# Expert weights fetched by SyncE at register addresses instead of by GpSimd gathers

## The chip, the cores and the metric

The kernel runs on one core of one Trainium2 chip. The core has five engines with instruction queues of their own: TensorE (PE in the profile, with PEld for the loading of its weights), VectorE (DVE), ScalarE (ACT), GpSimd (POOL) and SyncE (SP). Sixteen DMA engines serve all of them. A DMA is issued by an instruction in an engine's queue, and lands later. The metric is the device time of one execution in microseconds (us), as the median of several runs.

## The reference

One layer of a Perceiver in fp32. 256 latents of width 512 pass through three blocks, each added to the latents after a layernorm of its input:

1. Cross-attention to 4096 context rows and to the latents themselves: 16 query heads, 4 key and value heads of 128, RMS-normed queries and keys with rotary positions, softmax, output projection.
2. A Mamba-2 block: input projection, causal convolution of width 4, a state-space scan in chunks of 128, gated RMS norm, output projection.
3. A mixture of experts: 32 experts of inner width 192, of which each token uses six, and one shared expert of width 384.

Only the third block is touched. It computes

```python
scores = jax.nn.sigmoid(x @ gate_w)
topk_w, topk_i = jax.lax.top_k(scores, TOP_K)                     # 6 of 32
topk_w = topk_w / (jnp.sum(topk_w, axis=-1, keepdims=True) + 1e-20)
combine = jnp.sum(jax.nn.one_hot(topk_i, N_EXP) * topk_w[..., None], axis=1)
act = jax.nn.silu(jnp.einsum('td,edf->tef', x, wg)) * jnp.einsum('td,edf->tef', x, wu)
routed = jnp.einsum('tef,efd,te->td', act, wd, combine)
shared = (jax.nn.silu(x @ sg) * (x @ su)) @ sd
return routed + shared
```

Which tokens go to which expert is known only when the gate has been computed on the chip.

## The kernel before, in words

**Stages.** The cross-attention takes the context in chunks of 512 rows and fills most of the span (scores L748, exponentials L754, products with the values L774). The Mamba block follows. The experts' stage runs from about 807 us to the end.

**Slots.** The kernel computes a token's row only for the experts that it has chosen. The 32 experts are worked through as 16 pairs, one pair a round. Pairs 0 to 3 are experts 0 to 7, fixed when the kernel is built (`FIXED`). The other 24 experts are sorted into 24 slots (`NSLOT`) by how many tokens they have; `places` (L1250) finds the order with a few VectorE operations and a matmul whose result `ps_place` (L1267) holds, on every partition, the expert's number for each slot. Pairs 0 to 4 are wide: each expert has a block of 128 token rows. In pairs 5 to 15, the narrow ones, two experts share one block.

**Weights.** A pair's weights are three tiles: two of 128 x 2048 (1.05 MB each: gate, up, and the first 128 rows of down, of one expert each) and one `rest` tile of 128 x 512 (0.26 MB: the last 64 rows of down of both experts, one on each half of the partitions). There is room for six pairs (`NHELD`). `load_pair` (L1414) takes the place of the pair six before; in the loop it stands after the `down` that read that pair last. The tiles lie in memory that earlier stages used, so the trace calls them by old names (`w_in`, `w_out`, `lacc`, `wkv`, `ctx`, `v`, `kT`, `oacc`).

`load_weights` (L1402) loads the fixed pairs by plain DMAs of SyncE. For the others, `rows_at` (L1392) issues a gather on GpSimd: an indirect DMA that takes, for each of the 128 partitions, a row number from a column of a table in SBUF. The table `place` (128 x 36, unsigned) is made by `place_rows` (L1325): expert x 128 + partition for each of the 24 slots, and, for the 12 rest tiles, expert x 64 plus the partition folded into its half (`fold`, L1191). So there are three gathers a pair and 36 in all, 0.94 to 0.95 us of POOL each.

**A round.** TensorE transposes the block of token rows (`turn`, L1601), multiplies it with gate and up (`gate_up`, L237 in wide rounds, L1629 in narrow ones, into `ps_egu`); ACT takes the silu (L1631), VectorE multiplies it with the up half into `hid` (L1633, L1635); TensorE transposes that (`hidTp`, L1641) and multiplies with down (`ps_ye`, L1651, L1652, L1700); ACT copies the result to `y_sb`. For pairs 0 to 10 ACT then issues a DMA that stores `y_sb` to a buffer `ye` in DRAM (L1660 in narrow rounds): 16 stores of 256 KB. For pairs 11 to 15 `y_sb` stays in SBUF, and TensorE spreads it to the tokens with matmuls into `total` (L1670).

The token rows `xg_sb` come from a DRAM copy of the normed latents by gathers on GpSimd's queue (`fetch`, L1587). When the last store to `ye` has landed, 12 further gathers on that queue (`gather`, L1552, its DMA in L1557) bring the stored results `yk` back, one for each of two token tiles and six choices, and VectorE adds each to `x_sb` with its weight (`add`, L1565). Six tile buffers hold them, with two more borrowed for the last two. `finish` (L1811) adds `total`, and SyncE stores the output (L1814).

**What sets the order.** The source gives every engine its instructions in program order, but the framework's scheduler orders them anew by its own estimate of times, subject to data dependences and to `tc.issue_after(x)`, which keeps what stands under it behind `x`. Before the loop, the loads of pairs 4 and 5 are chained in this way behind the first token rows on GpSimd's queue (`begun`). Each DMA signals one of eight completion semaphores of its kind (eight for the hardware queues of SP and ACT together, eight for GpSimd's), taken in turn, and a DMA waits until the one eight before it in that turn has landed.

The loop over rounds, cut to what matters here:

```python
for n in range(NP):
    gate_up(n)
    ...
    if n + 1 < NP:
        main.turn(n + 1)
    if 0 < n <= LAST:
        down(n - 1)
    elif n > LAST:
        main.down_here(n - 1)
    ...
    if n >= NP - 3:
        add_behind(n, ...)
    if n > 0:
        load_pair(n - 1 + NHELD)
    ...
    turn_hidden(n)
```

Of the kernel before, what the change touches and what calls it, by code (L numbers as in the profile page):

```python
# [12 lines left out]
U32 = mybir.dt.uint32  # L13
I32 = mybir.dt.int32
AF = mybir.ActivationFunctionType
ALU = mybir.AluOpType
AX = mybir.AxisListType
PSUM = bass.MemoryType.PSUM

P = 128  # L20
L = 256
NT = L // P
# [24 lines left out]
NE = 32  # L47
FE = 192
FSH = 384
TOPK = 6  # L50
FT = FSH // P
REST = FE - P
# [4 lines left out]
FIXED = 8  # L57
HALFP = P // 2
# [3 lines left out]
HEAD = 4  # L62
EARLY = 4
TAIL = 10
NW = (FIXED + WIDES) // 2
LAST = NP - TAIL // 2
NSLOT = NE - FIXED
NB = FIXED + WIDES + (NSLOT - WIDES) // 2
NPL = NSLOT + NSLOT // 2
ZROW = (NW + LAST) * P  # L70
NOROOM = 2 * NE * P

# [12 lines left out]
def perceiver_layer(ctx: ExitStack, tc: tile.TileContext, a: dict, out: bass.AP):  # L85
    nc = tc.nc
# [63 lines left out]
    def layer(ctx, bounded):  # L150
# [16 lines left out]
        i8 = keep.tile([P, NT, 8], U32, name="i8")  # L167
        row = keep.tile([P, NT, TOPK], U32, name="row")
        row_y = keep.tile([P, NT, TOPK], U32, name="row_y")
        place = keep.tile([P, NPL], U32, name="place")  # L170
        listed = keep.tile([P, NB], U32, name="listed")
        token = keep.tile([P, NT], FP, name="token")
        crowded = keep.tile([1, 1], I32, name="crowded")
# [1 line left out]
        def carve(tl, *shapes):  # L175

            dims = " ".join(f"d{i}" for i in range(len(tl.shape) - 1))
            tl = tl if len(tl.shape) == 2 else tl.rearrange(f"p {dims} -> p ({dims})")
            out, at = [], 0
            for shape in shapes:  # L180
                n = int(np.prod(shape))
                v = tl[:, at:at + n]
                at += n
                if len(shape) == 2:
                    v = v.rearrange("p (a b) -> p a b", b=shape[1])
                elif len(shape) == 3:
                    v = v.rearrange("p (a b c) -> p a b c", b=shape[1], c=shape[2])
                out.append(v)
            assert at <= tl.shape[1]
            return out  # L190
# [114 lines left out]
        kv = {}  # L305
# [374 lines left out]
        for f in (of_heads[0], *key_turns[0:1], of_heads[1], *key_turns[1:2], last_first,  # L680
# [4 lines left out]
            turn = f()  # L685
# [488 lines left out]

        def routing_memory():
            r = carve(lacc[:, 1], (P,), (P,), (NT, NE), (NT, NE), (NT, NE), (NT, NE), (NT, NE), (NT, 8), (NT, 8),
                      (NT, TOPK), (NT, TOPK), (NT,), (NT * TOPK, NE), (FT, L), (1,), (NE,), (1,), (1,), (NE,), (NE,), (2, NE), (2,), (1,),
                      (NSLOT + 1,), (2, NSLOT + 1))
            names = ("iota", "before", "gate", "ev", "mask", "rank", "dst", "m8", "idx", "rowf", "w8", "den", "hot", "act",
                     "p", "free", "key", "pos", "keys", "at", "base", "value", "fold", "turn", "table")  # L1180
            m.update(zip(names, r))
            m["hot"] = m["hot"].rearrange("p (t k) e -> p t k e", t=NT)
            G.iota(m["iota"], pattern=[[1, P]], base=0, channel_multiplier=0, allow_small_or_imprecise_dtypes=True)
            G.iota(m["p"], pattern=[[0, 1]], base=0, channel_multiplier=1, allow_small_or_imprecise_dtypes=True)
            V.tensor_scalar(m["free"], ident[:, 0:NE], 1.0, None, ALU.mult)
            V.memset(m["free"][:, 0:FIXED], 0.0)
            V.tensor_tensor(m["before"], upper, ident, ALU.subtract)

        def place_tables():

            V.tensor_scalar(m["fold"], m["p"], float(HALFP), -float(HALFP), ALU.is_ge, ALU.mult)  # L1191
            V.tensor_tensor(m["fold"], m["fold"], m["p"], ALU.add)

            def steps(to, first, *by):
                to = to if len(by) == 1 else to.rearrange("p (a b) -> p a b", b=by[1][1])
                G.iota(to, pattern=[list(b) for b in by], base=first, channel_multiplier=0, allow_small_or_imprecise_dtypes=True)

            turn, rows, room, w = m["turn"], m["table"][:, 0], m["table"][:, 1], WIDES + 2 * MIXED
            for to, at0, step, more, narrow in ((turn, 0, 1, NSLOT - MIXED - WIDES, 1), (rows, FIXED * P, P, P - QUARTER, HALFP)):
                steps(to[:, 0:WIDES], at0, (step, WIDES))  # L1200
                steps(to[:, WIDES:w], at0 + WIDES * step, (step, MIXED), (more, 2))
                steps(to[:, w:NSLOT], at0 + (WIDES + MIXED) * step, (narrow, NSLOT - w))
            steps(room[:, WIDES:w], QUARTER, (0, MIXED), (P - HALFP, 2))
            V.tensor_scalar(rows[:, NSLOT:], m["p"], float(P), None, ALU.mult)
            G.memset(turn[:, NSLOT:], float(NSLOT))
            G.memset(room[:, 0:WIDES], 0.0)
            G.memset(room[:, w:NSLOT], float(HALFP))
            G.memset(room[:, NSLOT:], 0.0)
# [40 lines left out]

        def places(pc):  # L1250

            pos, key, keys, at, value, drawn = (
                m[n] for n in ("pos", "key", "keys", "at", "value", "dst"))
            n, low = NSLOT, slice(FIXED, NE)
            two = lambda ap, k: ap.unsqueeze(1).to_broadcast([P, 2, k])

            V.scalar_tensor_tensor(keys, pc[:, 0:NE], float(NE), m["iota"][:, 0:NE], ALU.mult, ALU.subtract)
            V.tensor_scalar(keys, keys, float(2 * NE), None, ALU.add)  # L1258
            V.tensor_tensor(at, keys, m["free"], ALU.mult)
            V.tensor_reduce(key, at, AX.X, ALU.add)  # L1260
            V.tensor_scalar(at[:, 0:n], keys[:, low], key, None, ALU.is_gt)
            V.tensor_reduce(pos, at[:, 0:n], AX.X, ALU.add)

            slot = at[:, 0:n + 1]
            V.tensor_scalar(slot, m["turn"], pos, None, ALU.is_equal)
            ps = bank("ps_place")
            TE.matmul(ps[:, 0:n], number, slot[:, 0:n], start=True, stop=True)  # L1267
            V.tensor_tensor(drawn[:, :, 0:n + 1], m["table"], two(slot, n + 1), ALU.mult)
            V.tensor_reduce(value, drawn[:, :, 0:n + 1], AX.X, ALU.add)
            V.tensor_tensor(drawn, two(ident[:, 0:NE], NE), value.unsqueeze(2).to_broadcast([P, 2, NE]), ALU.mult)  # L1270
            TE.matmul(ps[:, NE:3 * NE], ones, drawn.rearrange("p a b -> p (a b)"), start=True, stop=True)
            V.tensor_copy(expert, ps[:, 0:n])
            place_rows()
            V.tensor_copy(m["base"], ps[:, NE:3 * NE].rearrange("p (a b) -> p a b", b=NE))

        def result_rows():
# [40 lines left out]
        def list_early(es):  # L1317
# [3 lines left out]
                for t in range(NT):  # L1321
                    TE.matmul(ps[:, e:e + 1], first[:, t, e, :], token[:, t:t + 1], start=(t == 0), stop=(t == NT - 1))
            V.tensor_copy(listed[:, es.start:es.stop], ps[:, es.start:es.stop])

        def place_rows():  # L1325


            n, p = NSLOT, m["p"]
            V.tensor_scalar(place_f[:, 0:n], expert, float(P), p, ALU.mult, ALU.add)
            e2 = expert.rearrange("p (n i) -> p i n", i=2)  # L1330
            for i, half in enumerate((slice(0, HALFP), slice(HALFP, P))):
                V.tensor_scalar(place_f[half, n:], e2[half, i], float(REST), m["fold"][half], ALU.mult, ALU.add)
            V.tensor_copy(place, place_f)

        def picks(t, es):

# [52 lines left out]

        held, rests, weights = [], [], {}  # L1390

        def rows_at(out, src, c, by=place):  # L1392

            return G.indirect_dma_start(out=out, out_offset=None, in_=src,  # L1394
                                        in_offset=bass.IndirectOffsetOnAxis(ap=by[:, c:c + 1], axis=0)).ins
# [6 lines left out]
        def load_weights(to, n, fixed, behind=None):  # L1402

            if fixed:
                for i in range(2):
                    wait_for(nc.sync.dma_start(to[i], a["experts"][2 * n + i]), behind)
                nc.sync.dma_start(to[2], a["down_rest"][2 * n:2 * n + 2].rearrange("e p n -> (e p) n"))
            else:
                s = 2 * n - FIXED
                for i in range(2):  # L1410
                    rows_at(to[i], a["experts"].rearrange("e p n -> (e p) n"), s + i)
                return rows_at(to[2], a["down_rest"].rearrange("e p n -> (e p) n"), NE - FIXED + s // 2)

        def load_pair(n, behind=None):  # L1414
            if n < NP:
                k = n % NHELD
                weights[n] = (held[2 * k], held[2 * k + 1], rests[k])
                return load_weights(weights[n], n, 2 * n < FIXED, behind)

        def hold(*tiles, behind=None):  # L1420

# [30 lines left out]
        for fs in plan:  # L1452
# [44 lines left out]
        nc.sync.dma_start(xd[0:P, :], xn[:, 0, :])  # L1497
        assemble(1)
        n = NE - FIXED
        pick, number, expert, place_f, member, own, members = carve(  # L1500
            m["kv", 1], (NT * HEAD, P), (P,), (n,), (NPL,), (TAIL, NE), (TAIL, NE), (4 * TAIL,))
        pick = pick.rearrange("p (t e) r -> p t e r", t=NT)
        turn_latents = lambda t: turn_xn(t, bank("lnT"), halves=True)
        place_tables()
# [205 lines left out]
        with ExitStack() as rctx:  # L1710
# [37 lines left out]
            for n in range(2):  # L1748
                begun = main.fetch(n)
            for n in range(FIXED // 2, NHELD):  # L1750
                with tc.issue_after(begun):
                    begun = load_pair(n)
            copied = main.turn(0)
            with tc.issue_after(copied):
                rows_in_blocks(at)
# [155 lines left out]
```

## Time and profile before

| what | value |
|---|---|
| runs | 940.9, 943.85, 940.94 us; median 940.94 us |
| profiled execution | 946.23 us; span 944.3 us |
| TensorE busy | 924.2 us, 98% of the span |
| VectorE, ACT, POOL busy | 577.4, 370.0, 427.8 us |
| granted TensorE clock | 0.997 |
| bytes of POOL's queue (q0) and SP's queue (q1) | 39.59 MB and 77.43 MB |
| SP's wait for the last `x_sb` before the output store | 62.2 us |

The profile is one execution, recorded by the chip; its span goes from the first to the last instruction. A view of waits lists, for one engine, the idle time before its instructions and what ended it. A timeline row gives start, duration, engine, source line, operation, output and inputs, and in brackets the idle time before it. A row of a stretch gives the busy time of PE, PEld, DVE, ACT and POOL in it, the granted clock, the busy share of the DMA engines and GB/s.

### The profile page before, as it was taken

How to read it: one execution, taken by the hardware profiler on the slowest of the kernel's cores; microseconds unless marked ns; L12 is line 12 of the kernel's file. 1: busy time of each engine (PE TensorE's matmuls, PEld its weight loads, DVE VectorE, ACT ScalarE, POOL GpSimd, SP SyncE). 2: the span in 40 equal slices, each digit the busy share in tenths (PEclk: the TensorE clock that was granted, in tenths of full speed). 3: DMA queues.
4: the chain of work that ended last, by engine and by line, in shares of the span. 5: the costliest groups of instructions: out<-in, count | busy, mean ns of one | idle time of the engine just before them, and what ended most of it. 6: DMA issues, size and time to landing. Idle time of an engine off the chain costs nothing.

```text
span 944.3 us, 10567 instructions
## 1 busy us (share of the span) xinstructions
PE 924.2 (98%) x3266; PEld 504.9 (53%) x3266; DVE 577.4 (61%) x1199; ACT 370.0 (39%) x853; POOL 427.8 (45%) x498
## 2 busy tenths in 40 slices
PE   7999999999999999999999999999999999999996
PEld 3444555555555555555555555554465775654332
DVE  4866766566666665756666656658588685661224
ACT  4556444344344343443444434434154442022121
POOL 3769846345544644724725544220013251545542
PEclk9999999999999999999999999999999999999999
DMA  9651053053024114204305203090025481779983
GB/s 331 203 112 58 1 179 89 1 154 92 1 66 146 33 31 159 57 3 154 90 0 157 68 1 89 14 298 1 0 101 197 145 309 68 288 287 348 421 330 101
DMA packets 129716, 122.33 MB, mean 130 GB/s; under 512 B 79889, under 2 KB 99122, under 8 KB 124402
## 3 DMA queue, kind: packets, MB, share of 16 engines
q1 hardware_dynamic: 118960, 77.43, 27.2%
q0 software_dynamic: 7504, 39.59, 11.3%
q10 hardware_dynamic: 3186, 4.54, 1.3%
q8 instruction: 28, 0.46, 0.2%
q14 instruction: 38, 0.31, 0.1%
HBM read 89.54 MB, written 32.00 MB: 129 GB/s over the span
## 4 chain that ended last, share of the span: by engine, by line
PE 96%; DVE 2%; DMA 0%; issue 0%; ACT 0%; POOL 0%; SPq 0%; ACTq 0%
PE oT L774 24%; PE scT L748 24%; PE ps_kv L522 16%; PE ps_self L237 4%; PE ps_egu L1629 3%; PE ps_o L969 3%; PE ps_egu L237 3%; PE ps_first L399 3%; PE ps_xbc L237 2%; PE ps_out L1163 1%; PE ps_z L237 1%; PE xgTp L1601 1%; PE ps_ye L1651 1%; PE ps_ye L1652 1%; PE total L1670 1%; PE ps_ye L1700 1%
## 5 line engine op out<-in xcount | busy, mean ns | idle before, releaser
L765 DVE TENSOR_TENSOR lacc<-lacc,prT 128x512 f32<-128x512 f32 x256 | 199.8, 781 | 198.0 <-ACT prT L754 196.6
L754 ACT ACTIVATE prT<-scT,bq,rk 128x512 f32<-128x512 f32 x256 | 198.4, 775 | 280.9 <-PE scT L748 268.8
L748 PE MATMUL scT<-qT,kT 128*128 128x512 f32 x536 | 273.5, 592 | 0.0
L774 PE MATMUL oT<-prT,v 128*128 128x512 f32 x528 | 269.4, 592 | 0.0
L774 PEld LDWEIGHTS oT<-prT,v 128*128 128x128 f32 x528 | 100.2, 190 | 125.3 <-issue 118.6
L748 PEld LDWEIGHTS scT<-qT,kT 128*128 128x128 f32 x536 | 101.3, 190 | 41.4 <-issue 30.8
L522 PE MATMUL ps_kv<-fast,ctx 128*128 128x256 f32 x350 | 99.5, 379 | 0.0
L522 PEld LDWEIGHTS ps_kv<-fast,ctx 128*128 128x128 f32 x350 | 66.5, 190 | 47.9 <-issue 39.9
L471 POOL TENSOR_TENSOR ctx<-ctx 128x128 f32<-128x128 f32 x21 | 10.4, 495 | 98.7 <-PE ps_kv L522 98.7
L211 POOL TENSOR_TENSOR rk<-pv,mhalf 128x4 f32<-128x4 f32 x32 | 38.7, 1219 | 27.3 <-DVE pv L210 27.1
L522 PE MATMUL ps_kv<-wkv,ctx 128*128 128x256 f32 x168 | 48.8, 379 | 0.0
L282 ACT ACTIVATE xn<-kraw 128x128 f32<-128x128 f32 x112 | 33.5, 301 | 38.5 <-POOL kraw L497 21.5
L507 POOL TENSOR_TENSOR v<-fast,v 128x768 f32<-128x768 f32 x21 | 40.8, 1958 | 16.5 <-DVE fast L551 15.9
L522 PEld LDWEIGHTS ps_kv<-wkv,ctx 128*128 128x128 f32 x168 | 31.9, 190 | 28.2 <-issue 24.6
L780 DVE TENSOR_TENSOR oacc<-oT,oacc 128x512 f32<-128x512 f32 x64 | 43.7, 682 | 0.0
L1394 POOL DMA_INDIRECT xg_sb<-xd,listed x21 | 20.1, 959 | 31.7 <-DVE lacc L1258 14.4
L522 PE MATMUL ps_kv<-fast,fast 128*128 128x256 f32 x112 | 33.3, 379 | 0.0
L1633 DVE TENSOR_TENSOR hid<-si,ps_egu 128x128 f32<-128x128 f32 x11 | 3.2, 288 | 47.0 <-ACT si L1631 40.0
L522 PEld LDWEIGHTS ps_kv<-fast,fast 128*128 128x128 f32 x112 | 21.3, 190 | 17.8 <-issue 12.0
L288 DVE STREAM_TRANSPOSE tr<-kraw 128x512 f32<-128x512 f32 x28 | 18.3, 690 | 19.6 <-POOL kraw L496 19.6
L469 POOL TENSOR_TENSOR ctx<-fast 128x128 f32<-128x128 f32 x28 | 20.4, 730 | 19.6 <-PE ps_kv L522 19.1
L969 PE MATMUL ps_o<-wo,qT 128*128 128x512 f32 x64 | 28.8, 592 | 0.0
(423 smaller groups left out, 1399.9 us busy)
## 6 DMA issues: line engine op xcount, KB each, us to landing
xg<-xn SPq DMA_DIRECT2D x6, 2560.0 KB
ctx<-in_ctxT_dram SPq DMA_DIRECT2D x7, 1024.0 KB, 4.7
kd<-tr SPq DMA_DIRECT2D x112, 64.0 KB, 2.2
kT<-kd SPq DMA_DIRECT2D x28, 256.0 KB, 2.8
wq<-in_wq_dram SPq DMA_DIRECT2D x4, 1024.0 KB, 10.4
wo<-in_wo_dram SPq DMA_DIRECT2D x4, 1024.0 KB
w_in<-in_W_inT_dram SPq DMA_DIRECT2D x4, 1024.0 KB, 11.7
w_in<-in_experts_dram SPq DMA_DIRECT2D x4, 1024.0 KB, 6.9
```

The source lines that it names most:

```text
L211: return G.tensor_tensor(dst, v[:, :n], mhalf[:, :n], ALU.pow)
L237: last = TE.matmul(ps, lhs(k), rhs_of(k), start=(k == 0), stop=(k == KD - 1))
L282: S.activation(sq[:, h, :], raw[:, h, :], AF.Square, accum_out=ss[:, h:h + 1])
L399: TE.matmul(ps, lhs[:, j, k, :], rhs[:, k, :], start=(start and k == 0), stop=(k == 1), skip_group_check=True)
L507: G.tensor_tensor(to[:, 1:4], q, base[:, 1:4], ALU.add)
L522: TE.matmul(b[n], sets[name][i], y, start=start, stop=True, skip_group_check=True)
L748: scored.append(TE.matmul(sc, kT[:, g, i * P:(i + 1) * P], qT[:, t, heads4(g), :].rearrange("p h q -> p (h q)"), start=True, stop=True).ins)
L754: S.activation(pr, sc, AF.Exp, bias=shift, scale=SCALE if r is None else r[:, i, g:g + 1])
L765: V.tensor_tensor(la, la, pr, ALU.add)
L774: TE.matmul(outs[g, t], v[:, i, g * HD:(g + 1) * HD], pr, start=(n == 0), stop=last)
L780: V.tensor_tensor(ov, outs.pop((g, t)), ov, ALU.add)
L969: TE.matmul(m["ps_o", t], aT[:, t, h, :], wo[j][:, h % 4, :], start=(h == 0), stop=(h == NH - 1))
```

## The change

The table of row numbers goes. Instead the 24 expert numbers are copied as integers into a tile `drawn` on one partition. For each pair that is not fixed, SyncE loads two of these numbers into registers, and issues four DMAs whose DRAM address is computed from a register: two for the experts' large tiles and two for the halves of the rest tile. `load_pair` returns nothing any more, and the chain that held the first loads behind the token rows on GpSimd's queue is dropped with it. The fixed pairs' loads, the token rows and the result rows stay as they are. The local name `drawn` in `places` becomes `each`.

```diff
-        place = keep.tile([P, NPL], U32, name="place")
+        drawn = keep.tile([1, NSLOT], I32, name="drawn")
...
         def place_tables():
 
-            V.tensor_scalar(m["fold"], m["p"], float(HALFP), -float(HALFP), ALU.is_ge, ALU.mult)
-            V.tensor_tensor(m["fold"], m["fold"], m["p"], ALU.add)
...
+            V.tensor_copy(drawn, ps[0:1, 0:n])
             V.tensor_copy(expert, ps[:, 0:n])
-            place_rows()
             V.tensor_copy(m["base"], ps[:, NE:3 * NE].rearrange("p (a b) -> p a b", b=NE))
...
-        def place_rows():
-
-
-            n, p = NSLOT, m["p"]
-            V.tensor_scalar(place_f[:, 0:n], expert, float(P), p, ALU.mult, ALU.add)
-            e2 = expert.rearrange("p (n i) -> p i n", i=2)
-            for i, half in enumerate((slice(0, HALFP), slice(HALFP, P))):
-                V.tensor_scalar(place_f[half, n:], e2[half, i], float(REST), m["fold"][half], ALU.mult, ALU.add)
-            V.tensor_copy(place, place_f)
...
-        def rows_at(out, src, c, by=place):
+        def rows_at(out, src, c, by):
...
                 s = 2 * n - FIXED
-                for i in range(2):
-                    rows_at(to[i], a["experts"].rearrange("e p n -> (e p) n"), s + i)
-                return rows_at(to[2], a["down_rest"].rearrange("e p n -> (e p) n"), NE - FIXED + s // 2)
+                _, es = nc.values_load_multi_w_load_instructions(drawn[0:1, s:s + 2], engines=[mybir.EngineType.SP], min_val=0, max_val=NE - 1)
+                for i, e in enumerate(es):
+                    nc.sync.dma_start(to[i], a["experts"][bass.ds(e, 1)].rearrange("o p n -> (o p) n"))
+                for i, e in enumerate(es):
+                    nc.sync.dma_start(to[2][i * REST:(i + 1) * REST], a["down_rest"][bass.ds(e, 1)].rearrange("o p n -> (o p) n"))
...
-                return load_weights(weights[n], n, 2 * n < FIXED, behind)
+                load_weights(weights[n], n, 2 * n < FIXED, behind)
...
             for n in range(FIXED // 2, NHELD):
-                with tc.issue_after(begun):
-                    begun = load_pair(n)
+                load_pair(n)
```

More of the change, by code (lines that the diff above doesn't have):

```diff
@@ L68 @@
 NB = FIXED + WIDES + (NSLOT - WIDES) // 2
-NPL = NSLOT + NSLOT // 2
 ZROW = (NW + LAST) * P
@@ L1176, in routing_memory @@
             r = carve(lacc[:, 1], (P,), (P,), (NT, NE), (NT, NE), (NT, NE), (NT, NE), (NT, NE), (NT, 8), (NT, 8),
-                      (NT, TOPK), (NT, TOPK), (NT,), (NT * TOPK, NE), (FT, L), (1,), (NE,), (1,), (1,), (NE,), (NE,), (2, NE), (2,), (1,),
+                      (NT, TOPK), (NT, TOPK), (NT,), (NT * TOPK, NE), (FT, L), (1,), (NE,), (1,), (1,), (NE,), (NE,), (2, NE), (2,),
                       (NSLOT + 1,), (2, NSLOT + 1))
             names = ("iota", "before", "gate", "ev", "mask", "rank", "dst", "m8", "idx", "rowf", "w8", "den", "hot", "act",
-                     "p", "free", "key", "pos", "keys", "at", "base", "value", "fold", "turn", "table")
+                     "p", "free", "key", "pos", "keys", "at", "base", "value", "turn", "table")
             m.update(zip(names, r))
@@ L1250, in places @@
         def places(pc):
-            pos, key, keys, at, value, drawn = (
+            pos, key, keys, at, value, each = (
                 m[n] for n in ("pos", "key", "keys", "at", "value", "dst"))
@@ L1267, in places @@
             TE.matmul(ps[:, 0:n], number, slot[:, 0:n], start=True, stop=True)
[L1268 to L1271, printed above, removed]
+            V.tensor_tensor(each[:, :, 0:n + 1], m["table"], two(slot, n + 1), ALU.mult)
+            V.tensor_reduce(value, each[:, :, 0:n + 1], AX.X, ALU.add)
+            V.tensor_tensor(each, two(ident[:, 0:NE], NE), value.unsqueeze(2).to_broadcast([P, 2, NE]), ALU.mult)
+            TE.matmul(ps[:, NE:3 * NE], ones, each.rearrange("p a b -> p (a b)"), start=True, stop=True)
+            V.tensor_copy(drawn, ps[0:1, 0:n])
             V.tensor_copy(expert, ps[:, 0:n])
-            place_rows()
             V.tensor_copy(m["base"], ps[:, NE:3 * NE].rearrange("p (a b) -> p a b", b=NE))
@@ L1499, in layer @@
         n = NE - FIXED
-        pick, number, expert, place_f, member, own, members = carve(
-            m["kv", 1], (NT * HEAD, P), (P,), (n,), (NPL,), (TAIL, NE), (TAIL, NE), (4 * TAIL,))
+        pick, number, expert, member, own, members = carve(
+            m["kv", 1], (NT * HEAD, P), (P,), (n,), (TAIL, NE), (TAIL, NE), (4 * TAIL,))
         pick = pick.rearrange("p (t e) r -> p t e r", t=NT)
```

## The prediction

> **What bounds the kernel now.** I read the page's head first, then the chain that ended last, then TensorE's own waits in the expert stage, and only then the queues and engines that the edit touches.
>
> ```profile
> span 944.3 us, 10567 instructions
> PE 924.2 (98%) x3266; PEld 504.9 (53%) x3266; DVE 577.4 (61%) x1199; ACT 370.0 (39%) x853; POOL 427.8 (45%) x498
> PE 96%; DVE 2%; DMA 0%; issue 0%; ACT 0%; POOL 0%; SPq 0%; ACTq 0%
> ```
>
> TensorE is busy 98% of the span and carries 96% of the chain, so an edit that leaves its work alone can only give or take idle time between matmuls. Its waits from 798 us (the shared expert, routing and all rounds of experts) to the end are these (total, count, longest):
>
> ```profile
> PE total L1670 <- ACT y_sb L1665: 2.1, 1, 2.1
> PE ps_egu L1629 <- DVE xgT L1603: 1.2, 3, 0.4
> PE ps_egu L237 <- DVE xgT L1603: 1.2, 1, 1.2
> PE ps_shared L1384 <- issue: 0.4, 1, 0.4
> ```
>
> None names a weights transfer. That is so although the transfers run without a gap; by stretch (columns: us; busy PE, PEld, DVE, ACT, POOL; granted clock; DMA share; GB/s):
>
> ```profile
> 865.00:912.00 47.00, 45.55 (x348) 16.73 (x346) 9.67 (x30) 10.30 (x25) 22.10 (x25) 1.00 1.02 417
> ```
>
> A narrow round moves 2 x 1.05 + 0.26 MB of weights and 0.52 MB of token rows and results, 2.88 MB, at 417 GB/s 6.9 us, and lasts 5.6 us (two silus of ACT at 905.96 and 911.54). The queue therefore lives on its lead: over the twelve gathered pairs the landings are 5 to 13.5 us after the issue, and the smallest distance from landing to first matmul is 9.3 us (pair 13: 899.4 to 908.7).
>
> **The change part by part.**
>
> *Routing on VectorE.* Here are its rows before the first round, from the timeline (start, duration, what it does; in brackets the idle time before and what ended it), and the matmul that waits for them:
>
> ```profile
> 806.28 0.18 DVE L1272 COPY xc<-ps_place 128x24 f32<-128x24 f32 x1 [1.26 <-PE ps_place L1271]
> 806.51 0.27 DVE L1329 TENSOR_SCALAR xc<-xc,lacc 128x24 f32<-128x24 f32 x1
> 806.65 0.48 DVE L1332 TENSOR_SCALAR xc<-xc,lacc 64x12 f32<-64x12 f32 x2
> 807.30 0.17 DVE L1333 CAST place<-xc 128x36 uint32<-128x36 f32 x1
> 809.31 0.68 DVE L1603 COPY xgT<-xgTp 128x512 f32<-128x512 f32 x1
> 810.04 5.43 PE L237 MATMUL ps_egu<-w_in,xgT 128*128 128x384 f32 x16 [1.16 <-DVE xgT L1603]
> ```
>
> L1329, L1332 and L1333 go (0.27 + 0.48 + 0.17 = 0.92 us, overlapping), a 1x24 copy comes in ahead of L1272 (at most that row's 0.18). The xgT copy cannot start before its transposes (807.85 + 1.04 = 808.89), so at most about 808.95: 0.36 us sooner. Bounds: no gain, and the whole 1.16 us. I take -0.36, since the transposes are a recorded row. The two folding operations of L1191 and L1192 (0.15 us each at 724.9, beside other work) count nothing, at most -0.3.
>
> *Loads on SyncE.* Per pair it gets one load of two values (the load of `crowded` on SP: 0.29 us), register and assert steps (0.16 + 0.02 in that row; four, so 0.35), and four transfers with one register step each: 4 x (0.16 + 0.33, the fixed experts' mean issue) = 1.96. Together 2.6 us in a round of 5.6; twelve pairs take 31 us of an SP that otherwise waits 62.2 us for the last x_sb. Bounds: 0.33 x 4 = 1.3 and, with 0.29 for every step, 3.8 us; both are under 5.6. Pair 4 can start about 807 (806.28 + 0.18 + 0.29 + 0.35), against the first gather at 807.75. Queued behind it on SP are only the next pairs' loads; the `crowded` value, ready at 822.5, sits between pairs 6 and 7, whose buffers come free later. On TensorE: 0, covered by the 9.3 us lead; without it every late microsecond is one.
>
> The fixed experts' loads by SP from 754 to 762 us moved 356 GB/s, 430 in the best two microseconds. At 356 instead of 417 a round's 2.88 MB take 8.1 us, 1.2 more than now: over the seven pairs 9 to 15 8.4 us, still inside 9.3. Cost 0; bounds 0 and, with SP's 2.6 us on top, 8.4 + 2.6 - 9.3 = 1.7.
>
> *The rest tile in two.* Each pair's 0.26 MB becomes two transfers of 64 partitions: 12 more, 0.49 us of SP each, counted above. The Trainium skill, "DMA: Bandwidth & Descriptors", section "Rules for kernel authors", advises against just this: transfers to disjoint partition halves share the same engines and serialize, so one 128-partition transfer should be used. By its figure of about 2.0 us fixed per transfer ("Anatomy of one DMA"), served one after the other, 12 of them would be an estimated 24 us on a full queue, 15 past the lead, near 956 us. The rows speak otherwise, since two 1 MB loads issued 0.4 us apart keep the engines full: transfers in flight overlap, and bytes are unchanged. I take 0.
>
> *GpSimd.* 36 gathers of 0.95 us go, 34 us of POOL, and with them their places in the queue ahead of token rows and result rows. No wait of TensorE names POOL or a token row (those land at least 3.7 us early), so 0. After the first rounds this only matters in the tail.
>
> *Stores of ACT.* Hardware transfers share eight completion semaphores in turn, each waiting for the one eight before. 48 loads now alternate with ACT's 16 stores of y_sb. The closest meeting is pair 5's store behind pair 9's rest: about 861.5 + 10 = 871.5 against a store at 873.1. Behind the store on ACT's queue stands the next silu, with idle of 2.1 to 2.3 us before it. If that load takes 13.5 us (the slowest row) ACT is held 1.9 us. Bounds: 0, all of it inside the idle, and 11.4, none of it so in six narrow rounds; I take 0, by the idle rows, and price the case at half, 5.7.
>
> *The tail.* This is where order changes. TensorE needs `hid` of pairs 14 and 15 from VectorE. Before, pair 14's stands among the six additions of result rows; in the built changed kernel all six stand ahead of it, and the four of the second tile ahead of pair 15's now wait for the last four gathers rather than the next four. The timeline rows that decide, of ACT's queue, POOL, VectorE and TensorE:
>
> ```profile
> 903.61 0.33 ACTq L1660 DMA_DIRECT2D ye<-y_sb  x1
> 900.17 0.94 POOL L1394 DMA_INDIRECT ctx<-in_experts_dram,place  x1 [1.48 <-DMA v<-in_down_rest_dram,place]
> 911.83 0.95 POOL L1557 DMA_INDIRECT yk<-ye,row_y  x1 [8.21 <-DMA ye<-y_sb]
> 918.39 0.94 POOL L1557 DMA_INDIRECT yk<-ye,row_y  x1 [0.30 <-issue]
> 926.83 0.95 POOL L1557 DMA_INDIRECT yk<-ye,row_y  x1 [0.30 <-issue]
> 919.27 0.29 DVE L1633 TENSOR_TENSOR hid<-si,ps_egu 128x128 f32<-128x128 f32 x1 [3.26 <-issue]
> 923.02 0.38 PE L1641 MATMUL hidTp<-ident,hid 128*128 128x128 f32 x2
> 929.77 0.29 DVE L1633 TENSOR_TENSOR hid<-si,ps_egu 128x128 f32<-128x128 f32 x1 [1.35 <-ACT si L1631]
> ```
>
> Count from pair 10's store, 903.61. TensorE comes to pair 14's transpose 19.4 us later and, without the 2.06 us stall, to pair 15's 26.25 us later (931.92 - 2.06). The first row gather starts at T0, here 8.2. The sixth follows 6.56 later, lands in about 3.5 (3.1 to 3.8) and is added in 0.75: T0 + 10.8, with `hid` (0.65) T0 + 11.45. The twelfth follows 13.75 (eleven steps of 1.25) to 15.0 (seen) later: its addition ends at T0 + 18.0 to 19.3, with `hid` T0 + 18.65 to 19.95. With T0 = 8.2: 0.25 us late at pair 14, in all 0.6 to 1.9 at pair 15. With T0 under 6.3 nothing. T0 should be a little sooner, as pair 15's loads, gathers from 897.75 with the second one at 900.17 ahead of the store, now wait for pair 9's store, landing about 905.9; so less lies beside pair 10's store, whose 7.4 us compare with 2.0 for an equal store on quiet queues. Bounds 0 and, at the slowest store (10.3), 4.8; I take +0.4, near the low end of 0.6 to 1.9.
>
> *The 2.06 us stall* belongs to ACT starting a copy 3.4 us after its matmul. In the new order pair 15's gate matmuls (2.6 us) stand between, so such a stall would be hidden: 0 to -2.06. I take 0, since the profiled execution, 946.23 us (span 944.3 and 1.93 around it), is 5.3 above the median 940.94 and the stall may be part of those.
>
> Sum: 946.23 - 0.36 + 0 + 0.4 = 946.3 in the profiled execution; on the median 940.94, **941.0 us**.
>
> **The rivals.**
> - *Hidden anyway* (0.47): the edit does what it says, to work that already had 9 us of lead. 941.0; its own range goes from the whole front wait and no tail cost, 939.8, to the tail's 1.9, 942.5.
> - *VectorE's tail* (0.20, slower): pair 10's store lands late and both `hid` stand behind additions. Past T0 = 9.5 us after the store (at the slower pace) the loss passes 2.8; at a 10.3 us store T0 is 11.1 and the price 11.1 + 19.95 - 26.25 = 4.8, so 945.4. For it: the built order and saturated engines. Against: fewer bytes in flight beside that store.
> - *Stores held by loads* (0.11, slower): the shared semaphores above, to 940.94 - 0.36 + 5.7 = 946.3. For it: strict alternation of two engines' transfers. Against: 1.6 us of slack and ACT's idle.
> - *GpSimd relieved* (0.22, faster): T0 comes early, the 2.06 stall is hidden and the whole 1.16 us at the front goes: 940.94 - 3.2 = 937.7. For it: these are the stage's largest waits. Against: the stall may not exist in the median run.
>
> **How the numbers follow.** About 0.3%, 2.8 us, is what a measurement of this kernel can tell from no change. The first case gives "same", 0.47; the two slower ones 0.31; the last 0.22. The range reaches down to the last case and up to the tail's price, 937.6 to 945.4.
>
> **What would show it.** Right: no wait of TensorE for a weights transfer; the wait before the first gate matmuls near 0.8 us instead of 1.16; POOL about 34 us less busy; the software queue down by some 28 MB and SP's up by as much. T0 decides the tail: a transpose of `hid` (L1641 before) waiting for VectorE, with an addition ending last, makes the second case; silus late behind a held store the third. Wrong altogether would be weights arriving late, seen as waits of the gate matmuls for SP's transfers, or engines at well under 417 GB/s.

## The result: 0.57% slower, and the profile after

The changed kernel takes 948.69 us in the median of twenty runs, against 942.65 us for twenty of the kernel before (the 940.94 us that the prediction started from came from three): a ratio of 1.0057, with a 95% interval of 1.0043 to 1.0071. 941.0 us with a range up to 945.4 was forecast, that is no change; measured are 6.0 us more. The page of its profiled execution (949.46 us), its head, chain and the two queues:

```profile
span 947.7 us, 10759 instructions
PE 924.1 (98%) x3266; PEld 505.8 (53%) x3266; DVE 577.3 (61%) x1194; ACT 369.7 (39%) x853; POOL 392.9 (41%) x462
PE 92%; DMA 3%; DVE 3%; issue 1%; ACT 0%; POOL 0%; ACTq 0%; DVEq 0%
q1 hardware_dynamic: 124336, 105.75, 35.2%
q0 software_dynamic: 3088, 11.27, 3.8%
```

The 28 MB have moved from GpSimd's queue to SyncE's and POOL is 34.9 us less busy. TensorE does the same work, but the chain that ended last now runs through DMA and VectorE too. The waits of TensorE from 780 us on (total, count, longest) say where:

```profile
PE hidTp L1630 <- DVE hid L1622: 5.9, 1, 5.9
PE ps_egu L236 <- DVE xgT L1592: 0.8, 1, 0.8
```

The second line is the front: 0.8 instead of 1.16 us, the 0.36 us of the prediction. The first is new and is the loss: TensorE stands 5.9 us before it can transpose `hid` of pair 14. The timeline of the tail, of ACT's and SyncE's queues, POOL, VectorE and TensorE:

```profile
900.14 0.33 ACTq L1649 DMA_DIRECT2D ye<-y_sb  x1
906.47 0.33 SPq L1399 DMA_DIRECT2D ctx<-in_experts_dram  x1
908.72 0.94 POOL L1546 DMA_INDIRECT yk<-ye,row_y  x1 [15.64 <-DMA v<-in_down_rest_dram]
914.97 0.94 POOL L1546 DMA_INDIRECT yk<-ye,row_y  x1 [0.30 <-issue]
916.54 0.75 DVE L1554 SCALAR_TENSOR_TENSOR x_sb<-yk,lacc,x_sb 128x512 f32<-128x512 f32 x1 [6.66 <-DMA yk<-ye,row_y]
924.12 1.54 DVE L1554 SCALAR_TENSOR_TENSOR x_sb<-yk,lacc,x_sb 128x512 f32<-128x512 f32 x2 [0.25 <-DVE x_sb L1554]
925.57 0.28 DVE L1622 TENSOR_TENSOR hid<-si,ps_egu 128x128 f32<-128x128 f32 x1
925.91 0.83 PE L1630 MATMUL hidTp<-ident,hid 128*128 128x128 f32 x2 [5.90 <-DVE hid L1622]
```

The first row gather starts 8.6 us after pair 10's store, where 8.2 us had been seen before. But it lands 7.3 us after its issue, and the sixth 9.6 us (read from the updates of their semaphores), where those of before took 3.1 to 4.2 us (one of the twelve has no record). So the sixth addition ends T0 + 16.9 us and not T0 + 10.8, and `hid` of pair 14 stands behind it. Beside the gathers, pair 15's second large tile (`ctx`) is still on its way: issued at 906.47 instead of 900.17, landed at 922.2 instead of 913.2. Counted from pair 10's store it is issued 6.3 us behind instead of 3.4 us ahead.

After the wait TensorE comes back slower. By stretch (us; busy PE, PEld, DVE, ACT, POOL; granted clock; DMA share; GB/s), first the changed kernel, then the first two stretches of the kernel before:

```profile
865.00:890.00 25.00, 25.00 (x218) 9.31 (x220) 5.33 (x16) 6.21 (x15) 3.78 (x4) 1.00 1.03 391
890.00:905.00 15.00, 15.00 (x111) 5.67 (x104) 3.99 (x12) 2.71 (x7) 0.94 (x1) 1.00 1.03 368
926.00:930.00 4.00, 3.75 (x12) 1.51 (x14) 3.83 (x6) 0.37 (x1) 0.00 (x0) 0.50 0.22 72
```

```profile
865.00:890.00 25.00, 24.01 (x197) 8.53 (x196) 4.32 (x13) 5.11 (x12) 14.36 (x16) 1.00 1.02 418
890.00:905.00 15.00, 14.55 (x112) 5.42 (x113) 4.00 (x12) 3.67 (x9) 7.56 (x8) 1.00 1.03 419
```

The clock column reads 0.50 from 926 to 930; in the chain pair 15's sixteen gate matmuls take 4.50 us instead of 2.73. The first two rows of each hold a second surprise: the DMA engines are as busy as before (1.03; before 1.02 and 1.03), yet move 391 and 368 GB/s where the kernel before moved 418 and 419.

The sum of the tail, 5.9 + 0.24 (a short wait for `xgT`) + 1.8 (gate matmuls) + 0.45 (the two transposes, 0.83 instead of 0.38), is 8.4 us. Spans differ by only 3.4 us, since the profiled execution of before had itself lost some 3 us by the time it came to this transpose (923.02, against 920.0 here), and then its 2.06 us stall. The medians differ by 6.0, so an ordinary execution of the kernel before seems to lose some 2 us that the changed one does not. The profiles show a candidate. In that of the kernel before, ACT starts the silus of pairs 7, 8 and 9 only 2.1, 1.6 and 1.9 us after their gate matmuls have ended, and these three rounds, from 875 to 895 us, take 6.2 to 6.7 us instead of 5.6. Two such rounds stand in the profiles of e2 and e4 below, none in those of the changed kernel and of e10 (0.1 us). What holds ACT there is not shown.

### The profile page after: what moved, and what is told of

It reads as the page before. It is cut to its first block, busy times and chain, and to the rows that moved or that the text cites. A ratio compares the mean times of both kernels' runs of the same rounds, so it can differ in the third digit from the quotient of the medians.

```text
span 947.7 us, 10759 instructions
## 1 busy us (share of the span) xinstructions
PE 924.1 (98%) x3266; PEld 505.8 (53%) x3266; DVE 577.3 (61%) x1194; ACT 369.7 (39%) x853; POOL 392.9 (41%) x462
## 4 chain that ended last, share of the span: by engine, by line
PE 92%; DMA 3%; DVE 3%; issue 1%; ACT 0%; POOL 0%; ACTq 0%; DVEq 0%
PE oT L773 24%; PE scT L747 24%; PE ps_kv L521 16%; PE ps_self L236 4%; PE ps_o L968 3%; PE ps_egu L1618 3%; PE ps_egu L236 2%; PE ps_first L398 2%; PE ps_xbc L236 2%; PE ps_out L1162 1%; PE ps_z L236 1%; PE ps_ye L1689 1%; PE ps_ye L1641 1%; PE ps_sgu L236 1%; PE xgTp L1590 1%; PE ps_ye L1640 1%
## 5 line engine op out<-in xcount | busy, mean ns | idle before, releaser
L236 PE MATMUL ps_self<-wq,xT 128*128 128x512 f32 x64 | 28.6, 592 | 0.0
```

The source lines that it names most:

```text
L236: last = TE.matmul(ps, lhs(k), rhs_of(k), start=(k == 0), stop=(k == KD - 1))
```

## Experiments

The theory after the result: the loss needs two things at once, row gathers that land late since weights are still in flight, and an order of VectorE that puts `hid` behind the additions that wait for them. Rivals: the order alone, the lateness alone, SyncE's register work, something else in SyncE's transfers. The kernel before took between 940.1 and 943.1 us on the chips used, so ratios, each to the kernel before on the same chip, are compared.

**e1: the order put right.**

```diff
-                if n >= NP - 3:
-                    add_behind(n, *{NP - 3: (0, TOPK), NP - 2: (TOPK, 2 * TOPK - 2), NP - 1: (2 * TOPK - 2, 2 * TOPK)}[n])
+                if n >= NP - 2:
+                    add_behind(n, *{NP - 2: (0, TOPK), NP - 1: (TOPK, 2 * TOPK)}[n], turned)
```

(`turned` is the copy of the next pair's `xgT`; the additions are issued behind it as well.)

> The changed kernel with the additions of result rows put behind hid and the turned token rows: tile 0's six behind pair 14's hid and pair 15's xgT, tile 1's six behind pair 15's hid. Theory (late gathers times order): the 5.9 us wait of hidTp for hid goes, and with it the slower clock after it, about 2 us; 948.69 - 7.9 = about 940.8, ratio to before 0.996 to 1.000. Rival 1 (the order alone is to blame): the same number. Rival 2 (SyncE's transfers themselves cost TensorE time elsewhere): it stays at 947 or more, ratio 1.004 or more.

Measured: 942.46 us, ratio 1.0012 (0.9996 to 1.0027). TensorE's waits:

```profile
PE ps_egu L1618 <- issue: 1.3, 1, 1.3
PE ps_egu L236 <- DVE xgT L1592: 0.8, 1, 0.8
```

The wait for `hid` is gone, the clock stays at 1.00, and the loss is gone. Not all of the expected gain is there (0.996 to 1.000): the 1.3 us stand before the first gate matmul that reads `ctx` (921.40), so pair 15's late tile is now a wait of its own. The view of waits names no cause, but the instruction records do: TensorE's instruction at 921.40 waits for the semaphore that `ctx`'s transfer signals, and the last 8 KB packet of SyncE's loads ends at 920.63. SyncE's transfers cost nothing elsewhere that shows.

**e2: the changed order in the kernel before.**

```diff
+                if n >= NP - 2:
+                    with tc.issue_after(added[TOPK - 1 if n == NP - 2 else 2 * TOPK - 3]):
+                        return self.gated(n, si, ps)
```

(`gated` holds the multiplications that make `hid`, `added` the additions.)

> The kernel before, with hid of pair 14 held behind the six additions of tile 0 and hid of pair 15 behind four of tile 1, as the changed kernel has them. Theory: the gathers still land in 3.1 to 3.8 us, so the sixth addition ends 10.8 us after the first gather and the price is the 0.6 to 1.9 us of the prediction; ratio 1.000 to 1.003. Rival 1 (the order alone): the whole loss appears, about 6 us, ratio 1.006.

Measured: 944.54 us, ratio 1.0021 (1.0012 to 1.0031), a wait of 1.3 us for `hid` of pair 14. Its gathers land in 3.1 to 3.8 us. So the order alone, with gathers that land early, costs some 2 us (1.1 to 2.8 by the interval), close to the 0.6 to 1.9 that the prediction worked out, and not 6.

**e3: no weights beside the row gathers.** Pair 15's weights are not loaded, so that its result is another's.

```diff
+                if n < NP - 1:
-                load_weights(weights[n], n, 2 * n < FIXED, behind)
+                    load_weights(weights[n], n, 2 * n < FIXED, behind)
```

> The changed kernel without the loads of pair 15's weights (it multiplies with what pair 9 left), VectorE's order unchanged. Theory: no weights are in flight beside the result rows, gathers land in 3 to 5 us instead of 7.1 to 9.6, the wait for pair 14's hid falls from 5.9 us to under 1.5; ratio 0.998 to 1.001. Rival 1 (order alone): the wait stays near 5.9, ratio 1.006. Rival 3 (the first gather starts late because of the y stores): gathers land faster but the wait stays above 3 us.

Measured: 943.37 us, ratio 1.0011 (0.9996 to 1.0026). The gathers land in 3.1 to 4.1 us, although the first starts at 908.08 as in the changed kernel (908.72), and with the order unchanged the wait is

```profile
PE hidTp L1631 <- DVE hid L1623: 1.3, 2, 1.1
```

So T0 is not the cause; what lies beside the gathers is. e1, e2 and e3 together: either factor alone costs 0.1 to 0.2% (in e1 and e3 not clear of nothing), both 0.57%.

**e4: the kernel before with the additions behind `hid`** (the edit of e1).

> The kernel before with the additions behind hid as in the first run. Theory: before loses nothing to the additions, so nothing changes beyond the 2.1 us stall for y_sb that its profile shows: ratio 0.998 to 1.000. Rival 1: if order alone is worth much, 0.995 or less.

Measured: 945.9 us, ratio 1.0042 (1.0030 to 1.0055): slower, which neither theory had. TensorE has no new wait, and the output stores are issued 3.9 us earlier than in the profile of before (937.86), yet the span ends only 1.0 us sooner (two views, one line of each):

```profile
span 943.3 us, 10567 instructions
...
933.95 1.12 SPq L1814 DMA_DIRECT2D out_dram<-x_sb  x2
```

What comes last is GpSimd. In the instruction records its last gather, held back by the additions of tile 0 whose buffers it needs, lands at 931.9; then come 4.5 us of clean-up and a drain of 6.1 us to 942.5, while SyncE was done at 939.7. e10 tests that.

**e5 and e6: no registers; then one transfer fewer.** Constant addresses, so that other experts' weights are used, with four transfers a pair (e5), and with the rest tile in one of 128 partitions (e6):

```diff
-                for i, e in enumerate(es):
-                    nc.sync.dma_start(to[i], a["experts"][bass.ds(e, 1)].rearrange("o p n -> (o p) n"))
...
+                for i in range(2):
+                    nc.sync.dma_start(to[i], a["experts"][2 * n + i])
+                for i in range(2):
+                    nc.sync.dma_start(to[2][i * REST:(i + 1) * REST], a["down_rest"][2 * n + i])
```

In e6 the last two lines are

```diff
+                nc.sync.dma_start(to[2], a["down_rest"][2 * n:2 * n + 2].rearrange("e p n -> (e p) n"))
```

> The changed kernel with the same four SyncE transfers a pair from constant addresses, no values loaded into registers; experts are then taken by position instead of by the drawn order, so the weights are other experts' and the bytes the same. Theory: registers cost nothing on the path, so the loss stays: ratio 1.004 to 1.007, hidTp waits 4 to 7 us for hid. Rival (SyncE's register work makes the loads late): the loss goes, ratio 1.000 to 1.002.

> As the run before, but the rest tile of a pair in one transfer of 128 partitions, three a pair instead of four, same bytes. Theory (eight transfers in flight at most, so that four a pair hold the next ones back): the last load is issued 2 to 4 us earlier, the wait for hid falls to 2 to 4 us, ratio 1.002 to 1.004. Rival (bytes in flight alone, the count does not matter): like the run before, 1.004 to 1.007.

Measured: e5 948.81 us, ratio 1.0061 (1.0041 to 1.0082), a wait for `hid` of 5.8 us; the registers are not the cause. e6 943.91 us, ratio 0.9998 (0.9982 to 1.0014), better than the theory had said: no wait for `hid`, `ctx` issued at 900.46 (1.5 us behind pair 10's store), and the rate is back. Its tail still holds two other waits, 1.5 us for `xgT` and 1.2 us for `hidT`. The two stretches of e6:

```profile
865.00:890.00 25.00, 25.00 (x226) 9.31 (x224) 5.33 (x16) 5.99 (x15) 3.79 (x4) 1.00 1.03 418
890.00:905.00 15.00, 15.00 (x106) 5.94 (x104) 3.99 (x12) 3.57 (x9) 0.95 (x1) 1.00 1.02 415
```

(e5 moved 391 and 373.) But e6 takes away two things at once, the fourth transfer and the halves of 64 partitions. e13 parts them.

**e7 and e8: registers for the large tiles, gathers for the rest tiles,** in the changed order (e7) and with the additions behind `hid` (e8).

```diff
-                for i, e in enumerate(es):
-                    nc.sync.dma_start(to[2][i * REST:(i + 1) * REST], a["down_rest"][bass.ds(e, 1)].rearrange("o p n -> (o p) n"))
+                return rows_at(to[2], a["down_rest"].rearrange("e p n -> (e p) n"), s // 2, place)
```

> The changed kernel with the large tiles by SyncE as it has them, and the rest tiles by gathers of GpSimd as before (a table of 12 columns, four VectorE operations more); two hardware transfers a pair. VectorE's order in the tail is the changed one. Theory: SyncE is held back less, pair 15's second tile is issued near 900 instead of 906.5 and lands before most row gathers; the wait for hid falls under 2 us, ratio 1.000 to 1.002. Rival (hardware transfers beside row gathers slow these whatever their time): ratio 1.004 or more.

> The run before with the additions behind hid as in the first run. Theory: neither the wait for hid nor the 1.3 us wait that the first run has before pair 15's second gate matmuls remains: 940.8, ratio 0.997 to 0.999. Rival: something else bounds the tail, ratio 1.000 or more.

Measured: e7 942.17 us, ratio 0.9989 (0.9978 to 0.9999), `ctx` issued at 900.03, a wait for `hid` of 1.1 us. e8 939.31 us, ratio 0.9953 (0.9939 to 0.9968): faster than both kernels. Both ratios are a little better than expected. No wait above 0.3 us is left in e8's tail; the largest from 780 us on is the front's:

```profile
PE ps_egu L237 <- DVE xgT L1602: 1.1, 1, 1.1
```

So the registers and SyncE's queue are usable; the halved rest tile is what does not pay. e13 asks what about it.

**e13: four transfers, no halves.** As e6, with one large tile in two transfers of half the columns.

```diff
+                for j in range(2):
+                    nc.sync.dma_start(to[1][:, j * w:(j + 1) * w], a["experts"][2 * n + 1][:, j * w:(j + 1) * w])
```

> As e6 (constant addresses, rest tile in one transfer of 128 partitions; other experts' weights), with one of the two large tiles in two transfers of 128 partitions and half of the columns each: four transfers a pair as in e5, none of 64 partitions, same bytes. Theory A (the halves of 64 partitions slow the engines): 415 GB/s or more from 865 to 905 us, no wait for hid above 2 us, ratio 0.999 to 1.002, like e6. Theory B (four transfers a pair use up the eight in flight): rate near 370 to 390, wait for hid 4 us or more, ratio 1.004 to 1.007, like e5.

Measured: 941.5 us, ratio 0.9983 (0.9964 to 1.0003), no wait for `hid` (one of 2.4 us for `hidT`), and

```profile
865.00:890.00 25.00, 25.00 (x224) 9.42 (x220) 5.82 (x19) 5.69 (x15) 3.87 (x5) 1.00 1.03 414
890.00:905.00 15.00, 15.00 (x106) 5.82 (x100) 3.50 (x10) 3.24 (x8) 0.85 (x1) 1.00 1.03 412
```

That is Theory A, though rate and ratio lie just under its ranges: four transfers a pair cost nothing, the halves lower the rate. The packets' own times agree. Between 862 and 905 us an 8 KB packet of SyncE takes 0.344 us in the mean in the changed kernel, 0.315 in e6 and 0.314 in e13. How a half slows the others is not shown. In slices of 2 us the changed kernel's mean goes from 0.31 to 0.47, and packets of the halves move in the three slowest, 0.42 to 0.47 at 884, 900 and 908 us (28, 84 and 47 of them); but the slice with the most of them, 113 at 866 us, has 0.31. Nor are two properties of a half parted: it has 64 partitions, and it is small, 128 KB. No run loads the rest tile in two transfers of 128 partitions.

**e9, e12, e14, e15: is the slow clock part of the loss?** Matmuls whose result is overwritten fill TensorE's idle time in the changed kernel, 26 (e9) or 13 (e12, e14) of them; e15 is the changed kernel again.

```diff
+                if n == NP - 2:
+                    for _ in range(13):
+                        TE.matmul(tp.rearrange("p a b -> p (a b)"), ident, spread[:, 0, :], start=True, stop=True)
```

> The changed kernel with 26 matmuls of 128x256 (about 0.215 us each, 5.6 us) whose result is overwritten, put between the last total and the transpose of pair 14's hid, where TensorE otherwise idles 5.9 us. Theory (idle TensorE comes back at a lower granted clock, so pair 15's 16 gate matmuls take 4.5 instead of 2.7 us): the transposes start no later, the clock stays at 1.0 and 1.8 us come back; 946.9 against 948.7, ratio to before 1.003 to 1.005. Rival (the slow matmuls come from something else, as transfers into the tiles they read): they still take 4.5 us, ratio 1.006.

> The run before last but two with 13 matmuls instead of 26, as each proved to be two instructions of 0.215 us, so 5.6 us in all, just less than the 5.9 us of idle. Theory (idle TensorE comes back at a lower granted clock): pair 15's 16 gate matmuls take 2.7 us instead of 4.5 although the wait for hid ends when it did, and 1.8 us come back: 946.9 against 948.7, ratio to before 1.003 to 1.005. Rival (the clock falls anyway, or what is won is lost in a later wait): ratio 1.006.

> The kernel of e12, beside the changed kernel on one chip. Theory (idle TensorE comes back at a lower clock): 1.0 to 2.0 us less than e15. Rival: within 0.7 us of e15.

> The changed kernel itself, as the measure for e13 and e14 on their chip: ratio to before 1.005 to 1.008, wait for hid 5 to 7 us.

Measured: e9 950.91 us, ratio 1.0104 (1.0089 to 1.0120): I had mis-sized the filling, each matmul was two instructions, and 11.2 us of them outlasted the wait. e12 947.46 us, ratio 1.0075 (1.0061 to 1.0088): no gain in the whole time, against another chip's run of the changed kernel. Side by side it is there: e14 946.68 us, ratio 1.0044 (1.0031 to 1.0058), e15 949.16 us, ratio 1.0070 (1.0058 to 1.0082), 2.5 us apart and more than the expected 1.0 to 2.0. The clock itself is plain in the chain of e12 and of e15, the rows of pair 15's gate matmuls, first e12:

```profile
926.58 2.80 PE ps_egu L1618 x16
```

```profile
923.71 4.50 PE ps_egu L1618 x16
```

So this wait, 3.7 us in e15's profile (5 to 7 were expected; it is the fastest of the six runs of e15), costs 1.7 us more than itself. e12's trace also shows the landings of that tail without gaps; the issues from 905 to 930 us, with the time to landing last:

```profile
ctx<-in_experts_dram SPq DMA_DIRECT2D x1, 1024.0 KB, 15.0
v<-in_down_rest_dram SPq DMA_DIRECT2D x3, 128.0 KB, 11.9
yk<-ye,row_y POOLq DMA_INDIRECT x12, 8.2
```

**e10 and e11: GpSimd's end.** e4 and e8 with eight tile buffers for result rows, so that the last gathers need not wait for additions.

```diff
-            yp = rctx.enter_context(tc.tile_pool(name="yp", bufs=6))
+            yp = rctx.enter_context(tc.tile_pool(name="yp", bufs=8))
```

> The kernel before with the additions behind hid, as in the fourth run, and eight tile buffers for result rows instead of six, so that the last row gather need not wait for the sixth addition. Theory (in the fourth run GpSimd's own end, some 14 us after its last gather, came last): the last gather goes 3 to 6 us earlier, GpSimd's end falls below that of the output store, ratio 0.996 to 1.000 instead of 1.0042. Rival (the order itself costs something on TensorE): ratio stays at 1.003 or more.

> The eighth run with eight tile buffers for result rows. GpSimd's end there stands 0.4 us behind nothing but just ahead of the output store. Theory: TensorE's chain bounds it, so nothing changes, ratio 0.994 to 0.997. Rival (GpSimd's end decides in most executions): 0.993 or less.

Measured: e10 940.55 us, ratio 0.9998 (0.9989 to 1.0007): the last gather goes at 923.69 instead of 928.35, and e4's loss is gone. GpSimd's end, 2.8 us behind SyncE's in e4 (942.5 against 939.7), was the larger part of it. It need not be all: e10's profile also lacks the two late rounds of e4's, some 1.5 us. e11 938.58 us, ratio 0.9979 (0.9969 to 0.9989), just outside the expected 0.994 to 0.997: faster than the kernel before, like e8, and not faster than e8 by the ratios; their chips differ, so between these two nothing is decided.

## Why the prediction was wrong, point by point

- **The rest tile in two, taken as 0**, is the step that failed first. I argued that transfers in flight overlap and the bytes are the same. They are, but the halves lower the rate, from 418 and 415 GB/s in e6 and 414 and 412 in e13 to 391 and 373 in e5 and 391 and 368 in the changed kernel. "Engines at well under 417 GB/s" stood among the signs of being wrong altogether, and a lower rate had been priced (356 GB/s), but only against the lead of the weights. The lower rate makes the last weights late: SyncE issues `ctx` 6.3 us behind pair 10's store, where the prediction's landing of pair 9's store (905.9) allowed 2.3 and e6 has 1.5. How it is held is shown by its own waits from 860 to 912 us, of which these are the largest:

```profile
SPq L1401 <- DMA w_in<-in_experts_dram: 8.3, 3, 4.9
SPq L1401 <- DMA ye<-y_sb: 5.6, 4, 3.5
SPq L1399 <- DMA oacc<-in_experts_dram: 4.6, 1, 4.6
SPq L1399 <- DMA ye<-y_sb: 4.5, 1, 4.5
```

  SyncE waits for earlier transfers to land, eight back in the turn of the semaphores (a half of pair 13's rest tile is issued at 896.85, as pair 12's second large tile lands at 896.84), so a lower rate becomes a later issue. The Trainium skill's rule that was weighed there ("DMA: Bandwidth & Descriptors", "Rules for kernel authors": use one 128-partition transfer instead of two to disjoint halves) was right in its direction: the runs show a lower rate with the engines as busy as before. The estimate of 24 us made from its page was not right: the figure of about 2.0 us stands there for transfers that GpSimd issues, these are SyncE's, and e13 with four transfers a pair loses nothing against e6 with three. Why packets slow beside the halves, no run here shows.
- **The tail, taken at +0.4 with an upper end of 4.8**, is the term of the sum that was too small: 8.4 us in the profile. It had the right mechanism, order before `hid`, and a wrong entry: "lands in about 3.5". That came from gathers with little beside them (DMA share 0.62 from 912 to 926 us, against 0.90 in the changed kernel). I saw that pair 15's loads would move away from pair 10's store, and missed that they would move beside the gathers. 7.3 to 9.6 us, in place of 3.5, is the missing 6 us of T0 + 16.9. T0 itself, 8.6 us after the store, was not early as I took it to be, and stayed under the 9.5 us that I had named as the point of decision.
- **The rival "VectorE's tail" (0.20)** is the one that came, by another door: slow gathers, not a late store. Its price of 4.8 also left out the clock: 1.8 us on the gate matmuls.
- **The front** was right: 0.36 us.
- **SyncE's issue work and registers, taken as 0**: right (e5 with constant addresses loses as much). The 2.6 us a pair never reached TensorE.
- **GpSimd, taken as 0**: nearly right; it is 34.9 us less busy, and that moved no wait in the tail. But the token rows that "land at least 3.7 us early" are late once, early in the stage: TensorE waits 0.36 us for `xg_sb` at 826.25 (1.2 us in e3, 1.3 in e9), where the kernel before has no such wait. A gather issued for it at 819.54 takes some 7 us to land, with SyncE's loads in flight; its like before took some 5.
- **ACT's stores held by loads (0.11)**: did not come: pair 10's store is issued 0.6 us after its copy begins, as before, and the silus of pairs 5 to 13 start within 0.1 us of their matmuls' end. The waiting is on the other side, where SyncE waits for stores.
- **The lead of 9.3 us on weights** was more than used up by pair 15. No wait of TensorE names weights in the changed kernel, but only since TensorE was waiting for `hid` at that time: without that wait, in e1, it stands 1.3 us for `ctx`.

## What to carry to other kernels

When transfers are moved, ask not only whether their own user still gets them in time, but what else is in flight when they now run: a latency taken from a quiet stretch of the trace doesn't hold beside them. Be wary of splitting a small tile by halves of the partitions: here a large tile split by columns (e13) and a gather for the small one (e7) kept the rate. Look at GB/s beside the busy share of the engines, since the share alone showed no difference. Where a scheduler orders the queues, read its order for work that waits for DMAs ahead of work that the busiest engine needs, and pin that order: e8 and e11, with large tiles at register addresses, rest tiles gathered and the additions pinned behind `hid`, beat both kernels.

## What the runs showed of the hardware that was not expected

- Two transfers of 64 partitions, 128 KB each, among 1 MB ones: 391 and 368 GB/s at a DMA share of 1.03; the same bytes in transfers of 128 partitions, none under 256 KB: 412 to 418 at 1.02 to 1.03.
- After 5.9 us of idle, and in e15 after 3.7, TensorE's sixteen gate matmuls took 4.50 us instead of 2.73; in the changed kernel the clock granted from 926 to 930 us was 0.50. After the 2.06 us stall of the kernel before they took 2.73. The Trainium skill, "TensorE: Matmul & The Clock Gate", section "What's actually happening", puts the step to half clock at about 3.4 us of idle; these three waits agree with it. A half clock came without such idle too: in the profiles of both kernels the clock is also 0.50 for 3.4 us, from 818.5 us before and from 817.8 us in the changed one, behind 24 matmuls of 17 columns and with no wait above 1.2 us since 800 us. Eight gate matmuls there take 3.84 us in the kernel before; in e8 the same eight take 2.82 and the clock stays at 1.00, behind the same 24. What decides it, no run here shows.
- GpSimd's end grows with the DMAs that it has issued: the last long drain took 6.12 us in the kernel before (69 gathers in the stage), 4.16 in e8 (45) and 3.18 in the changed kernel (33), some 0.08 us a gather. In e4 that end came last.
